# Output projection of the last but one attention unit: pairs of parts and seven products in place of plain matmuls

## The chip, the cores and the metric

The kernel runs on one core of a Trainium2 chip. The metric is the device time of one execution in microseconds; the median of several runs is given. The core has five engines with a queue each, worked in order: TensorE (PE; its weight loads are shown apart as PEld), VectorE (DVE), ScalarE (ACT), GpSimd (POOL) and SyncE (SP), which issues most DMAs. Everything is float32.

## The reference

One transformer layer with a norm after each half, on x of shape (2, 512, 512): grouped attention with 32 query heads, 8 key and value heads of width 128, rotary positions and a causal mask, then a feed-forward half that is a base matrix with a mixture of low-rank experts.

```python
q = hidden_states @ Wq + bq            # 32 heads of 128
k = hidden_states @ Wk + bk            # 8 heads
v = hidden_states @ Wv + bv
q, k = _rope(q, pos), _rope(k, pos)
scores = einsum('bgrsd,bgtd->bgrst', qg, k) / sqrt(128)
probs = softmax(where(causal, scores, min))
ctx = einsum('bgrst,bgtd->bgrsd', probs, v)
x = _layernorm(x + ctx @ Wo + bo)
y = x @ W_base.T + b_base
contribs = einsum('bter,eor->bteo', x @ A[active], Bm[active]) * 2
alpha = softmax(log(prior) + logits)   # router
x = _layernorm(x + y + sum_e contribs * alpha)
```

The change concerns `ctx @ Wo`, summed over the heads.

## The kernel before

**Units, parts, slots.** The attention is cut into 16 units, one for each pair of key head and batch element (4 query heads each), and each unit into 4 parts of 128 query rows: 64 parts, numbered p, four a unit. Parts 56 to 59 are unit 14, the last but one; parts 60 to 63 are unit 15, taken in the order of rows 2, 3, 0, 1. A part is worked in four slots, one score matmul each: slot T belongs to part T // 4, so there are 256 score slots. The function `slot(T)` writes out, by hand and in order, what every engine does in slot T. The schedule is manual: each engine takes its instructions in exactly that order, and semaphores order the engines among each other. Functions put in the table `extra` by `put(slot, f)` come at the end of their slot, in the order in which they were put there.

**What a part goes through.** Scores on TensorE (`score`, slot T); masked maximum on VectorE and exponentials on ScalarE one slot later; reciprocal, normalising and the transposes into `zt` up to slot T + 4; the transposed blocks are stored to DRAM (`blocks_out`, four DMAs on SP at slot 4p + 7) and read back as `pT` (`blocks_in`, one DMA on SP at slot 4p + 9, waiting for those four to land). The weighing with v (`weigh`) starts at slot 4p + 12 and takes as many slots as the part has key blocks, one matmul each; ScalarE then writes the context `ctxT` (`context_out`). There are two score banks: a score needs the bank of the score two slots earlier, which is free when its exponentials are done.

**Wo by pairs.** For units 0 to 13 the product of context and Wo is taken for two parts at once: the 2 x 2 blocks of the pair (two parts by two halves of the heads) times the 2 x 2 blocks of Wo (two halves of the heads by two halves of the columns), with seven block products in place of eight (`wo_products`, steps 0, 1, 2, 3, 4, 6, 7 in slots 21 + 8k + step for pair k). They need sums of weight blocks (`wo_sums`, four for each set of weights, on VectorE; the third overwrites a block of Wo in place), and sums of context blocks (`ctx_sums`, four for each pair, on POOL, one buffer). The products go into two PSUM banks, wx and wy. After a step, VectorE adds 256 columns from a bank to `x_sb` (`wo_adds`, seven adds a pair), one slot after the step. Most steps add into a bank that still holds the sum of earlier steps, so a step waits until the add that reads the earlier state is done.

**Wo plainly.** For units 14 and 15 each part has four matmuls over 512 columns (`wo_mm`), two in each of two slots listed in `plain_at`, and then one add of 512 columns (`wo_out`). Parts 56 to 59 take slots 246 to 251, 253 and 254; part 60 takes 256 and 257, part 61 takes 261 and 262; parts 62 and 63 come in the code after the loop.

**What else lies there.** At slot 237 the memory of the projections is closed and that of the FFN (`ffn_pool`) opened. Between slots 237 and 262 the base weights are loaded and transposed, and the FFN of the first batch element is woven in: `stats` at 238, 239 and 245, inverse roots by Newton steps at 240 and 245 (`newton`: four small VectorE operations, then twelve small POOL operations), `centre` at 246 and 247 on VectorE, transposes at 248 and 249, the base product at 250 and 251 for the first tile, `logits` and `alphas` (the router's softmax) at 252, `low_rank` at 253, `finish` and `add` at 254; the same for the next tiles from 256 and 258. The last Wo load (`load_wo`, 1 MB on SP) is put in slot 246.

Of the kernel before, what the change touches and what calls it, by code (L numbers as in the profile page):

```python
# [9 lines left out]
F32 = mybir.dt.float32  # L10
# [19 lines left out]
def postln_layer_kernel(  # L30
# [33 lines left out]
    nc = tc.nc  # L64
    B, S, HID = x.shape
    NT = B * S // P
    TPB = S // P
# [20 lines left out]
    NSETS = len(sets)  # L88
# [4 lines left out]
    def set_of(u):  # L93
        return u // B if u < MIXED else MIXED // B + u - MIXED
# [294 lines left out]
    def k_mm(u, c):  # L389
        g, b = unit(u)  # L390
        proj_mm(("k", u), ps_k, "k", wqk["k", g], slice(0, D), b, c)
# [43 lines left out]
    def strassen_sums(engine, a11, a12, a21, a22, s1, s2, s4):  # L435

        engine.tensor_tensor(s1, a21, a22, ALU.add)  # L437
        engine.tensor_tensor(s2, s1, a11, ALU.subtract)
        engine.tensor_tensor(s4, a12, s2, ALU.subtract)
        engine.tensor_tensor(a21, a11, a21, ALU.subtract)  # L440
# [6 lines left out]
    def product(ps, wt, xt, start):  # L447

        for c in range(CH):
            nc.tensor.matmul(  # L450
                ps, lhsT=wt[:, c, :], rhs=xt[:, c, :], start=start and c == 0, stop=c == CH - 1,
                skip_group_check=True)
# [177 lines left out]
    wt = {}  # L630
# [3 lines left out]
    def wo_block(n, c_half, n_half):  # L634
        return wos[n][:, CH * c_half : CH * (c_half + 1), ts(n_half, NHALF)]

    def wo_sums(n, step):

        if step == 0:
            shape = [P, 3, CH, NHALF]  # L640
            if n == NSETS - 4:
                wt[n] = late["pool"].tile(shape, F32, name="wt_late")
            else:
                wt[n] = wow.tile(shape, F32, tag="wt", name=f"wt_{n}", bufs=1)
        t1, t2, t4 = (wt[n][:, m] for m in range(3))
        b11, b12, b21, b22 = (wo_block(n, c_half, n_half) for c_half in range(2) for n_half in range(2))
        nc.vector.tensor_tensor(
            *((t1, b12, b11), (t2, b22, t1), (b12, b22, b12), (t4, b21, t2))[step], ALU.subtract)

    def ctx_block(k, head, c_half):  # L650
        return ctxT[2 * k + head][:, CH * c_half : CH * (c_half + 1), :]

    def ctx_sums(k):
        c = cs[k] = work.tile([P, 3, CH, P], F32, tag="cs", name=f"cs_{k}", bufs=1)
        strassen_sums(
            nc.gpsimd, *(ctx_block(k, h, c_half) for h in range(2) for c_half in range(2)), *(c[:, n] for n in range(3)))

    def wo_products(k, step):
        n = set_of(parts[2 * k][0])
        if step == 0:  # L660
            pw[k, "x"] = ps_wo.tile([P, NHALF], F32, tag="wx", name="wx")
            product(pw[k, "x"], ctx_block(k, 0, 0), wo_block(n, 0, 0), True)
        elif step == 1:
            pw[k, "y"] = ps_wo.tile([P, NHALF], F32, tag="wy", name="wy")
            product(pw[k, "y"], ctx_block(k, 0, 1), wo_block(n, 1, 0), True)
        elif step == 2:
            product(pw[k, "x"], cs[k][:, 1], wt[n][:, 1], False)
        elif step == 3:
            product(pw[k, "y"], cs[k][:, 0], wt[n][:, 0], True)
        elif step == 4:  # L670
            product(pw[k, "x"], ctx_block(k, 1, 0), wo_block(n, 0, 1), False)
        elif step == 6:
            product(pw[k, "x"], ctx_block(k, 1, 1), wt[n][:, 2], False)
        elif step == 7:
            product(pw[k, "y"], cs[k][:, 2], wo_block(n, 1, 1), False)

    def wo_add(k, bank, head, n_half):
        u, i = parts[2 * k + head]
        into = x_sb[:, unit(u)[1] * TPB + i, ts(n_half, NHALF)]
        nc.vector.tensor_tensor(into, pw[k, bank], into, ALU.add)  # L680

    def wo_adds(k, step):
        for bank, head, n_half in {
            1: (("x", 0, 0),), 2: (("y", 0, 0),), 3: (("x", 0, 1),), 4: (("y", 1, 1),),
            5: (("x", 1, 1),), 7: (("x", 1, 0),), 8: (("y", 0, 1),),
        }.get(step, ()):
            wo_add(k, bank, head, n_half)

    def wo_mm(p, r):

        u, i = parts[p]
        if r == 0:
            pwo[p] = ps_wo.tile([P, HID], F32, tag=("wx", "wy")[p % 2], name="po")
        nc.tensor.matmul(  # L694
            pwo[p], lhsT=ctxT[p][:, r, :], rhs=wos[set_of(u)][:, r, :], start=(r == 0), stop=(r == R - 1))
# [180 lines left out]
    NP = len(parts)  # L876
# [3 lines left out]
    LAG_WO = 21  # L880
    LAST = QB * TPB * (NU - 2)
# [3 lines left out]
    def put(slot, f):  # L885
        extra.setdefault(slot, []).append(f)
# [36 lines left out]
    late = {}  # L923
# [10 lines left out]
    def kv_at(T):  # L934

        frame, o = divmod(T - KV_FROM, UNIT)
        p, k = divmod(frame + B, VG * B)
        kind, b = "kv"[k // B], k % B
        if 0 < p < G // VG and (kind, p, b) != ("v", 1, 0):
            return (kind, p, b), o  # L940
        return None, None
# [16 lines left out]
            weigh_at.setdefault(QB * p + LAG_CTX + j + (p == NP - 2), []).append((p, j))  # L958


    plain_at = {}
    free = LAST + LAG_WO + 1
    for p in range(NP - 2 * TPB, NP):
        free = max(free, QB * p + LAG_CTX + parts[p][1] + 2)
        for step in range(2):
            plain_at[free + step] = p, step
        free += 2

    def slot(T):

        uq, step = divmod(T + 24, UNIT)
        kq, step = divmod(step, 8)
        now = 0 < uq < NU
        if now and step != 7 and step != 4:
            q_products(uq, kq, {0: 2, 1: 6, 2: 5, 3: 7, 5: 4, 6: 3}[step])
        un, kn = (uq, 1) if kq == 0 else (uq + 1, 0)
        if un < NU and step == 7:
            q_products(un, kn, 1)
        uk, l = divmod(T + UNIT, UNIT)
        if 0 < uk < PLAIN_K and l < KC:  # L980
            k_mm(uk, l)
        kv, o = kv_at(T)
        if kv and o in KV_STEPS:
            kv_products(*kv, KV_STEPS[o])
        kw, sw = divmod(T - LAG_WO, 8)
        products = 0 <= kw < LAST // 8
        if products:
            wo_products(kw, sw)
        plain = plain_at.get(T)
        if plain:  # L990
            p, step_o = plain
            wo_mm(p, 2 * step_o)
            wo_mm(p, 2 * step_o + 1)
        if 0 <= T < T_END:
            score(T)
        for part, j in weigh_at.get(T, ()):
            weigh(part, j)

        if now and step in (0, 2, 4, 6):
            q_copy(uq, kq, ("p1", "u2", "u3", "c21")[step // 2])  # L1000
        if kv and KV_OUT.get(o) in KV_ON_ACT:
            kv_out(*kv, KV_OUT[o])
        for part, j in weigh_at.get(T - 1, ()):
            if j == parts[part][1]:
                context_out(part)

        if 0 <= T - 3 < T_END:
            normalise(T - 3)
        if 0 <= T - 1 < T_END:
            masked_max(T - 1)  # L1010
            exponentials(T - 1)
        if products:
            wo_adds(kw, sw)
        if sw == 0 and 0 < kw <= LAST // 8:
            wo_adds(kw - 1, 8)
        if now and step in (1, 5, 7):
            q_sum(uq, kq, {1: "p1", 5: "u3", 7: "u2"}[step])
        if kv and o in KV_OUT and KV_OUT[o] not in KV_ON_ACT:
            kv_out(*kv, KV_OUT[o])
        if 0 <= T - 2 < T_END:  # L1020
            reciprocals(T - 2)
        if 0 <= T - 4 < T_END:
            blocks_transposed(T - 4)
            if (T - 4) % QB == QB - 1:
                blocks_out((T - 4) // QB)
        if T % QB == 1 and 0 <= T // QB - 2 < NP:
            blocks_in(T // QB - 2)
        if 0 <= (T - LAG_WO + 1) // 8 < LAST // 8 and (T - LAG_WO + 1) % 8 == 0:
            ctx_sums((T - LAG_WO + 1) // 8)

        ur, sr = divmod(T + 24 - 7, UNIT)
        kr, sr = divmod(sr, 8)
        if 0 < ur < NU and sr < 6:
            q_rope(ur, 2 * kr + (sr < 3), sr % 3)
        k_slots = (4, 5, 6) if uk < PLAIN_K else (11, 13, 14) if uk < NU - 1 else (3, 5, 6)
        if 0 < uk < NU and l in k_slots:
            k_rope(uk, k_slots.index(l))
        if plain and step_o:
            wo_out(p)
        for f in extra.pop(T, ()):  # L1040
            f()
# [88 lines left out]
        slot(T)  # L1130
    proj_stack.close()
    ffn_pool = ctx.enter_context(tc.tile_pool(name="ffn", bufs=1))
    wb_sb = ffn_pool.tile([P, OC, HID], F32, name="wb_sb")
    wbT = ffn_pool.tile([P, KC, 2, WX_COLS], F32, name="wbT")
    nc.gpsimd.tensor_copy(wbT[:, :, 0, OH : OH + ARH], arT[:, :, :ARH])
# [184 lines left out]
```

## Time and profile before

| | |
|---|---|
| median of 3 runs | 817.26 us (816.86 to 817.88) |
| the profiled execution's own time | 816.9 us |
| its span, first to last instruction | 815.1 us |
| granted TensorE clock | 0.998 |
| TensorE, VectorE, ScalarE, POOL busy | 99%, 75%, 47%, 42% of the span |
| plain Wo in the profile: matmul records, adds | 64 records, 8 adds of 692 ns |
| Wo by pairs: adds of 256 columns | 420 ns each |
| context sums on POOL, 128x256 | 740 to 837 ns mean |

A float32 matmul leaves two records in the profile. The records of TensorE overlap[...]; the chain of work that ended last shows by how much each moves the time on, as start, length, engine, tile and number of records. In lists of instructions a bracket gives the idle time ahead of an instruction and what ended it. Tiles: wx and wy are the banks of Wo by pairs, po those of plain Wo, sc scores, pc the weighing, tp transposes, py the FFN.

### The profile page before, as it was taken

How to read it: one execution, taken by the hardware profiler on the slowest of the kernel's cores; microseconds unless marked ns; L12 is line 12 of the kernel's file. 1: busy time of each engine (PE TensorE's matmuls, PEld its weight loads, DVE VectorE, ACT ScalarE, POOL GpSimd, SP SyncE). 2: the span in 40 equal slices, each digit the busy share in tenths (PEclk: the TensorE clock that was granted, in tenths of full speed). 3: DMA queues.
4: the chain of work that ended last, by engine and by line, in shares of the span. 5: the costliest groups of instructions: out<-in, count | busy, mean ns of one | idle time of the engine just before them, and what ended most of it. 6: DMA issues, size and time to landing. Idle time of an engine off the chain costs nothing.

```text
span 815.1 us, 11389 instructions
## 1 busy us (share of the span) xinstructions
PE 807.0 (99%) x3457; PEld 609.7 (75%) x3457; DVE 609.8 (75%) x1978; ACT 384.9 (47%) x1074; POOL 338.6 (42%) x392
## 2 busy tenths in 40 slices
PE   9999999999999999999999999999999999999996
PEld 7887777777777778777777778777777878656575
DVE  4778877687879886787867876787888689973455
ACT  2355454444545454545435454544545454663244
POOL 8666645421444345322443245343464333420033
PEclk9999999999999999999999999999999999999999
DMA  9025736355455637264544637365453726674211
GB/s 298 26 72 143 219 83 202 91 130 156 134 169 136 182 93 219 77 181 129 147 147 121 178 82 219 91 160 179 137 146 91 232 66 181 189 263 143 77 39 65
DMA packets 84415, 116.00 MB, mean 142 GB/s; under 512 B 6525, under 2 KB 64237, under 8 KB 82306
## 3 DMA queue, kind: packets, MB, share of 16 engines
q1 hardware_dynamic: 83154, 114.71, 49.0%
q8 instruction: 27, 0.44, 0.2%
q10 hardware_dynamic: 752, 0.42, 0.2%
q14 instruction: 34, 0.28, 0.1%
q0 software_dynamic: 448, 0.14, 0.1%
HBM read 71.21 MB, written 44.04 MB: 141 GB/s over the span
## 4 chain that ended last, share of the span: by engine, by line
PE 96%; POOL 1%; DVE 1%; ACT 1%; issue 0%; POOLq 0%
PE pc L618 17%; PE sc L562 15%; PE qx L450 14%; PE wx L450 12%; PE qy L450 10%; PE wy L450 9%; PE kx L450 4%; PE vx L528 4%; PE po L694 3%; PE py L788 3%; PE pv L348 3%; PE pp L365 1%; PE tp L285 1%; PE py L829 1%; POOL zt L191 0%; POOL act_er L220 0%
## 5 line engine op out<-in xcount | busy, mean ns | idle before, releaser
L577 ACT ACTIVATE p<-sc,nmax 128x288 f32<-128x288 f32 (+15 forms) x256 | 124.2, 485 | 197.7 <-DVE nmax L570 175.2
L570 DVE CUSTOM_DVE_ANT_0 sc<-sc,maskw 128x288 f32<-128x288 f32 (+15 forms) x256 | 114.2, 446 | 136.3 <-PE sc L562 134.7
L618 PE MATMUL pc<-pT,v 128*128 128x512 f32 x320 | 165.3, 599 | 0.0
L562 PE MATMUL sc<-kT,qT 128*128 128x160 f32 (+15 forms) x512 | 161.7, 398 | 0.3 <-ACT p L577 0.3
L386 POOL TENSOR_TENSOR qT<-q,t 128x512 f32<-128x512 f32 x64 | 88.0, 1376 | 176.1 <-DVE q L385 165.0
L585 ACT ACTIVATE p<-p,den 128x288 f32<-128x288 f32 (+15 forms) x256 | 133.2, 521 | 0.0
L562 PEld LDWEIGHTS sc<-kT,qT 128*128 128x128 f32 x512 | 96.1, 190 | 21.9 <-issue 8.1
L625 ACT ACTIVATE ctxT<-pc,bqkT 128x512 f32<-128x512 f32 x64 | 44.0, 688 | 114.8 <-PE pc L618 114.7
L437 POOL TENSOR_TENSOR cs<-ctxT 128x256 f32<-128x256 f32 x28 | 22.4, 801 | 158.5 <-PE wy L450 95.4
L593 DVE STREAM_TRANSPOSE zt<-p 128x128 f32<-128x128 f32 (+2 forms) x192 | 81.7, 426 | 0.0
L486 ACT COPY q<-qx 128x256 f32<-128x256 f32 x128 | 47.4, 370 | 51.4 <-PE qx L450 49.8
L618 PEld LDWEIGHTS pc<-pT,v 128*128 128x128 f32 x320 | 57.1, 190 | 18.7 <-issue 5.7
L450 PE MATMUL qx<-xs,wq 128*128 128x256 f32 x256 | 66.3, 381 | 0.0
L450 PEld LDWEIGHTS qx<-xs,wq 128*128 128x128 f32 x256 | 47.3, 190 | 23.2 <-issue 18.4
L595 DVE STREAM_TRANSPOSE zt<-p 128x32 f32<-128x32 f32 (+3 forms) x256 | 57.6, 225 | 0.0
L450 PE MATMUL wx<-wo,ctxT 128*128 128x256 f32 x224 | 57.5, 379 | 0.0
L378 DVE SCALAR_TENSOR_TENSOR t<-q,bqkT,rope_sb 64x512 f32<-64x512 f32 x64 | 52.3, 818 | 3.5 <-ACT q L486 1.7
L381 DVE SCALAR_TENSOR_TENSOR t<-q,bqkT,rope_sb 64x512 f32<-64x512 f32 x64 | 50.3, 786 | 1.5
L577 ACT ACTIVATION_READ_ACCUMULATOR p<-sc,nmax 128x1 f32 x256 | 49.8, 194 | 0.0
L385 DVE SCALAR_TENSOR_TENSOR q<-q,bqkT,rope_sb 128x512 f32<-128x512 f32 x64 | 48.1, 751 | 0.1
L450 PEld LDWEIGHTS wx<-wo,ctxT 128*128 128x128 f32 x224 | 42.5, 190 | 7.0 <-issue 1.4
L680 DVE TENSOR_TENSOR x_sb<-wx,x_sb 128x256 f32<-128x256 f32 x112 | 47.0, 420 | 0.0
(234 smaller groups left out, 1468.3 us busy)
## 6 DMA issues: line engine op xcount, KB each, us to landing
db<-zt SPq DMA_DIRECT2D x64, 256.0 KB, 4.3
pT<-db SPq DMA_DIRECT2D x16, 1024.0 KB, 4.8
db<-zt SPq DMA_DIRECT2D x64, 192.0 KB, 3.3
pT<-db SPq DMA_DIRECT2D x16, 768.0 KB, 4.4
wq<-in_L_attn_Wq_dram SPq DMA_DIRECT2D x20, 512.0 KB, 5.1
wo<-in_L_attn_Wo_dram SPq DMA_DIRECT2D x10, 1024.0 KB, 9.0
db<-zt SPq DMA_DIRECT2D x64, 128.0 KB, 2.4
pT<-db SPq DMA_DIRECT2D x16, 512.0 KB, 4.2
```

What stands on the lines that cost most here:

```text
L378: nc.vector.scalar_tensor_tensor(t2[lo, :], q[hi, :], b_ap[hi, :], rope_sb[hi, 1, :], ALU.add, ALU.mult)
L381: nc.vector.scalar_tensor_tensor(t2[hi, :], q[lo, :], b_ap[lo, :], rope_sb[lo, 1, :], ALU.add, ALU.mult)
L385: nc.vector.scalar_tensor_tensor(t1, q, b_ap, rope_sb[:, 0, :], ALU.add, ALU.mult)
L386: nc.gpsimd.tensor_tensor(dst, t1[:, :].rearrange("p (n s) -> p n s", s=BLK), t2[:, :].rearrange("p (n s) -> p n s", s=BLK), ALU.add)
L450: nc.tensor.matmul(ps, lhsT=wt[:, c, :], rhs=xt[:, c, :], start=start and c == 0, stop=c == CH - 1, skip_group_check=True)
L562: nc.tensor.matmul(sc[s][:, :w], lhsT=qT[u][:, i * QB + n].rearrange("p r s -> p (r s)"), rhs=kT[u][:].rearrange("p n s -> p (n s)")[:, :w ...
L570: nc.vector.tensor_tensor_reduce(sc[s][:, :w], sc[s][:, :w], maskw[:, S - w :], -SCALE, -MASKED, ALU.add, ALU.min, nmax[s])
L577: nc.scalar.activation(ptile[s][:, :w], sc[s][:, :w], AF.Exp, bias=nmax[s], scale=-1.0, accum_out=rden[s])
L585: nc.scalar.activation(ptile[s][:, :w], ptile[s][:, :w], AF.Copy, scale=rden[s])
L593: nc.vector.transpose(z[:, :, last - i : last, n, :].rearrange("p q j s -> p j q s"), ptile[s][:, : i * P])
L595: nc.vector.transpose(z[:, : n + 1, last, n, :], ptile[s][:, i * P : w])
L618: nc.tensor.matmul(psc[p], lhsT=v_sb[g // VG, b][:, j, ts(g % VG, D)], rhs=pT[p][:, :, ts(j, P)], start=(j == 0), stop=(j == i))
```

## The change

Unit 14 (parts 56 to 59, two pairs, numbers 28 and 29) takes Wo by pairs too.

- The plain products and adds of parts 56 to 59 go away; `plain_at` keeps parts 60 to 63. Part 60 moves from slots 256 and 257 to 257 and 258; part 61 stays.
- Pair 28 takes slots 247 to 251 with one step each (0 to 4) and slot 252 with steps 6 and 7. Pair 29 takes slot 253 with steps 0 and 1, 254 with 2 and 3, 255 with 4, 256 with 6 and 7.
- For these two pairs, `wo_adds` come in the same slot as their step; for the earlier pairs they come one slot after it, as before.
- `ctx_sums` of the two pairs, four POOL operations each, are put at slots 246 and 252.
- `wo_sums` of unit 14's weights, four operations, are put on POOL at slots 242, 243, 245 and 246, into a tile `wt_last` of the FFN's memory. As they are put earlier in the code, they stand ahead of what other functions put in the same slot; in slot 245 that is the second `newton`, and in slot 246 the context sums come ahead of the fourth weight sum.
- The steps of the earlier pairs are now read from a table (`wo_at`, `adds_at`) and keep their slots.

```diff
-    def wo_sums(n, step):
+    def wo_sums(n, step, engine=nc.vector):
...
+            elif n == NSETS - 2:
+                wt[n] = late["ffn"].tile(shape, F32, name="wt_last")
...
-        nc.vector.tensor_tensor(
+        engine.tensor_tensor(
             *((t1, b12, b11), (t2, b22, t1), (b12, b22, b12), (t4, b21, t2))[step], ALU.subtract)
...
+    WO_PAIRS = (NP - TPB) // 2
+    wo_at = {}
+    for k in range(WO_PAIRS - 2):
+        for step in (0, 1, 2, 3, 4, 6, 7):
+            wo_at[8 * k + LAG_WO + step] = (k, (step,))
+    LAST_PAIRS = LAST + LAG_WO + 2
+    for n, steps in enumerate(((0,), (1,), (2,), (3,), (4,), (6, 7))):
+        wo_at[LAST_PAIRS + n] = (WO_PAIRS - 2, steps)
+    for n, steps in enumerate(((0, 1), (2, 3), (4,), (6, 7))):
+        wo_at[LAST_PAIRS + 6 + n] = (WO_PAIRS - 1, steps)
+
+    adds_at = {}
+    for T, (k, steps) in wo_at.items():
+        for step in steps:
+            adds_at.setdefault(T + (k < WO_PAIRS - 2), []).append((k, step + 1))
+    for n in range(2):
+        put(LAST_PAIRS + 6 * n - 1, lambda n=n: ctx_sums(WO_PAIRS - 2 + n))
+    for step in range(4):
+        put(LAST_PAIRS + (-5, -4, -2, -1)[step], lambda step=step: wo_sums(NSETS - 2, step, nc.gpsimd))
+
     plain_at = {}
-    free = LAST + LAG_WO + 1
-    for p in range(NP - 2 * TPB, NP):
+    free = LAST_PAIRS + 10
+    for p in range(NP - TPB, NP):
         free = max(free, QB * p + LAG_CTX + parts[p][1] + 2)
...
-        kw, sw = divmod(T - LAG_WO, 8)
-        products = 0 <= kw < LAST // 8
-        if products:
-            wo_products(kw, sw)
+        kw, steps_w = wo_at.get(T, (0, ()))
+        for step_w in steps_w:
+            wo_products(kw, step_w)
...
-        if products:
-            wo_adds(kw, sw)
-        if sw == 0 and 0 < kw <= LAST // 8:
-            wo_adds(kw - 1, 8)
+        for k, read in adds_at.get(T, ()):
+            wo_adds(k, read)
...
     ffn_pool = ctx.enter_context(tc.tile_pool(name="ffn", bufs=1))
+    late["ffn"] = ffn_pool
```

## The prediction

> **What bounds the kernel now.** I read the page first, for each engine's busy time, then the chain of work that ended last around the changed slots, then the timelines of SP, VectorE and POOL there. Page:
>
> ```profile
> PE 807.0 (99%) x3457; PEld 609.7 (75%) x3457; DVE 609.8 (75%) x1978; ACT 384.9 (47%) x1074; POOL 338.6 (42%) x392
> ```
>
> TensorE is never free, so its work and its waits make the time. The chain shows what a piece of work costs there (start, length, what); the slots that change begin at 721.71:
>
> ```profile
> 711.73 0.86 PE wx L450 x4
> ...
> 721.71 1.72 PE po L694 x4
> 723.42 0.81 PE sc L562 x2
> 724.23 0.86 PE pc L618 x2
> 725.09 0.44 PE tp L285 x4
> 725.53 1.72 PE po L694 x4
> 727.24 0.86 PE sc L562 x2
> 728.10 1.72 PE po L694 x4
> 729.82 0.14 PE sc L562 x2
> 729.96 0.94 PE pc L618 x2
> ```
>
> One product of a pair is 0.86 us (four records); half a plain part is 1.72, so a part is 3.44. In this stretch every piece begins where the one before ended: here TensorE alone set the pace. The slots can be read off: 246 starts at 721.71, 247 at 725.53, 248 at 728.10; further down the same view, 249 at 731.77, 252 at 744.74, 255 at 752.70, 256 at 753.13.
>
> **The change, part by part.**
>
> *TensorE's work.* Removed: 4 plain parts x 3.44 = 13.76 us. Added: 2 pairs x 7 products x 0.86 = 12.04. Balance -1.72 us, which is -0.21% of 815.1. That is the whole prize; whatever wait appears comes off it.
>
> *Where the work lies.* Before, slots 246 to 251, 253 and 254 each held 1.72 of plain product, and 256 and 257 held part 60. After: 246 nothing; 247 to 251 one product (0.86); 252, 253, 254 two (1.72); 255 one; 256 two; part 60 in 257 and 258. So TensorE first runs ahead of the old schedule by 1.72 + 0.86 + 0.86 = 3.44 us at the end of slot 248's products, by more until 251, and pays it back from 252 on. Running ahead is where it can meet data that is not there. I walked each slot with the old durations and asked which partner is late.
>
> *First wait: slot 248, the load of pT for part 59.* Without waits: slot 246 is 0.81 + 0.86 + 0.44, to 723.82; slot 247 is 0.86 + 0.86, to 725.54; slot 248's product ends at 726.40, its score at 726.54. Then the weighing of part 59 needs its pT. SP issues that load here:
>
> ```profile
> 723.24 0.34 SPq L611 DMA_DIRECT2D pT<-db  x1
> 723.67 0.40 SPq L162 DMA_DIRECT2D wo<-in_L_attn_Wo_dram  x1
> ```
>
> ```profile
> pT<-db SPq DMA_DIRECT2D x16, 1024.0 KB, 4.8
> ```
>
> The load is issued once part 59's block stores (issued at 716.73, slot 243, before anything changed) have landed; nothing in the change moves it forward. It lands at 723.24 + 4.8 = 728.04. Before, the weighing began at 729.96 and never saw it; now TensorE waits 728.04 - 726.54 = 1.5 us. [...] I take the row, a load of the same size on the same queue[...]. ScalarE's exponentials of slot 246, which free the score bank of 248, end near 726.5 by their old lengths (wb copy, context, normalising, exponentials), 0 to 0.3 us late, inside this wait.
>
> *The middle, 249 to 254.* Weighing 59 now starts 729.96 - 728.04 = 1.92 us ahead of the old time. Slots 249 to 251 save 0.86 each (4.50 ahead at 252), 252 gives back 1.72 (2.78 ahead at 253 and 254). Part 60's load was issued at 734.65, lands in 4.3, so by 739.0, or 0.6 later because one extra add precedes its stores on VectorE; needed at 742.2. Part 61's stores follow an add at 737.8 and go out at about 738.8 against 738.44 before, its load lands near 750, needed near 754. Both hidden, by 2.6 and 4 us.
>
> *POOL.* Added: 4 weight sums on 128x512 and 8 context sums on 128x256. The rows nearest to the first have the same shape and engine:
>
> ```profile
> L429 POOL TENSOR_TENSOR xs<-xT x2: 1275/1494/1712, 29.3 to 32.2; 128x512 f32<-128x512 f32 x2
> L429 POOL TENSOR_TENSOR xs<-xT,xs x2: 1598/1688/1779, 30.7 to 36.4; 128x512 f32<-128x512 f32 x2
> ```
>
> So 1.3 to 1.8 each; the context sums are 0.73 to 0.93 (3.2 a pair in the timeline, gaps included). The first three weight sums stand ahead of the second Newton root of the norms:
>
> ```profile
> 722.66 0.20 POOL L737 TENSOR_TENSOR t<-rstd_a 128x2 f32<-128x2 f32 x1 [6.91 <-DVE rstd_a L735]
> ```
>
> POOL was idle for 6.91 us there; 3 x 1.8 = 5.4 fit, so Newton still starts at 722.66 and ends at 726.35. Pair 28's context sums follow to 729.6, the fourth weight sum to 731.4. Step 2 (slot 249, at 729.85) needs the second context sum, done near 728.1; step 6 (slot 252, about 740) needs the fourth weight sum. [...] Newton's steps beside the two centrings at 723.62 took 0.38 instead of 0.20. The other two centrings (0.99 us) will meet the context sums[...]. Uncovered, each us is a us. Pair 29's context sums start after step 7 of pair 28 (ends near 741.9), second done by 743.7, needed at 746.1. The new tile lies in memory whose last projection user on POOL ended at 706.9, so I cost it nothing; if it had to wait, the bound is POOL's same 1.5 us of spare before Newton slips.
>
> *VectorE's adds.* 14 x 0.42 = 5.9 us for 4 x 0.69 = 2.8: +3.1 us on an engine that idled up to 3.44 us at a time before these plain adds. Hidden as work, +3.1 if not. Their place matters more: from pair 28 on, a slot's adds come in the same slot, and the next product into that bank waits for them. Pair 29 packs two steps a slot, so one add stands between slots with the FFN's work ahead of it in VectorE's order.
>
> *Second wait: slot 256.* Step 6 of pair 29 adds into the bank that step 4 (slot 255) filled, so it waits for that bank's add, and ahead of it on VectorE are the finish of the first FFN tile (slot 254) and slot 254's masked maximum:
>
> ```profile
> 752.30 0.86 DVE L839 TENSOR_TENSOR y<-py,x_sb 128x256 f32<-128x256 f32 x2 [0.98 <-PE py L829]
> 753.20 0.69 DVE L713 BATCH_NORM_STATS2 st<-y 128x6 f32<-128x512 f32 x1
> ...
> 754.02 0.37 DVE L570 CUSTOM_DVE_ANT_0 sc<-sc,maskw 128x224 f32<-128x224 f32 x1
> ```
>
> The finish's matmuls start at 751.84 in the chain; VectorE has done the maximum at 754.31, 2.47 later, and the add would end 0.42 later, 2.89 after. Now the finish starts 2.78 earlier, at 749.06; the add ends at 751.95. TensorE is through the finish (0.86), step 4 (0.86) and the score (0.43) at 751.21, so it waits 0.74, plus 0.05 for the signal and 0.2 of restart (a product that had waited for such an add took 1.07 instead of 0.86, at 708.87): 1.0 us. Queued behind it on TensorE: step 7, the weighing and the FFN base, so all later work.
>
> *Sum.* -1.72 + 1.5 + 1.0 = **+0.8 us**. After 258 the old order returns and TensorE stays full to 801, so no later gap absorbs it. Profiled execution: span 815.1, to 815.9. Its own time was 816.9, 1.8 above its span; the median 817.26 is 2.16 above. The prediction moves the median: 817.26 + 0.8 = **818.1**.
>
> **Rivals.**
> *All of the gain:* pT lands early and the add is in time. For it: TensorE was the only limit before. Against: the load's issue and the add's place above. 817.26 - 1.7 = 815.5.
> *One wait only:* the load's, 817.1, or the add's, 816.5. For it: both margins, 1.5 and 0.7 us, are sums of many short pieces.
> *A third wait, slower than before:* slot 254, step 2 of pair 29 needs the add of step 0, which stands behind the router's softmax of the first tile (1.45 us from 744.78 to 746.23 in the old timeline, with a ScalarE step in it) and behind the last add of pair 28. I get that add done near 744.9 and TensorE there at 746.1: 1.2 us to spare. From 1.2 late on it decides; an equal slip again costs 1.2, 819.3.
> *It changes nothing because other work hides TensorE:* excluded by the 99%.
>
> **How the numbers follow.** 0.2% is 1.63 us, about what a measurement of this kernel can tell from no change: the bounds are 815.63 and 818.89. Chances: two waits 0.52 (own range 817.4 to 819.0), one wait 0.20, all gained 0.05, a third wait or longer ones 0.23. Faster: the 0.05. Slower: the 0.23 and 0.04 from the upper end of the two-wait case. Same: the rest, 0.68. The range leaves out the full gain and the far end of the third wait: 816.2 to 820.0.
>
> **What would show it.** Right: fourteen 0.86 products and no plain product before part 60; a TensorE wait on the pT load near 726.5 of about 1.5 us, one on the x_sb add near 751 of about 1 us; Newton still starting near 722.7. Wrong: no wait at either place, weight sums over 2.3 us each that push Newton back, or a wait on POOL's sums at steps 2 or 6.

## The result, and the profile after

| | before | after |
|---|---|---|
| median | 817.25 us (816.83 to 817.94, 15 runs) | 819.31 us (817.74 to 824.38, 15 runs) |
| ratio of the medians, 95% interval | | 1.003 (1.0017 to 1.0044) |
| profiled execution, span | 815.1 us | 822.6 us |
| granted TensorE clock there | 0.998 | 0.994 |

The change costs 2.1 us. The forecast was 818.1, the range 816.2 to 820.0. The shortest execution of after, 817.74, is 0.9 above the shortest of before, close to the forecast step of 0.8; the median is 1.2 above the forecast value. The spread belongs to the result: before, 15 executions lay within 1.1 us, after they lie within 6.6. The clock sorts them without exception: the eight executions with a mean granted clock of 0.998 or more took 817.74 to 819.31, the seven with 0.997 or less took 820.25 to 824.38. So the median is the longest execution of the first group. The profiled one is the longest of all, so the lines below show the costs at their largest.

Busy times, on the page:

```profile
PE 809.7 (98%) x3481; PEld 617.2 (75%) x3481; DVE 612.6 (74%) x1988; ACT 384.9 (47%) x1074; POOL 349.0 (42%) x404
```

TensorE's busy time is up by 2.7 us, although 1.72 us of work were taken away: part of its work ran longer. The chain of work that ended last shows where (start, length, what):

```profile
723.66 0.77 PE pc L618 x2
724.43 6.89 DMA pT<-db
...
731.37 2.07 PE pc L618 x2
733.44 1.71 PE tp L285 x8
735.15 1.71 PE wx L450 x4
...
755.64 0.45 PE py L831 x2
...
758.26 0.29 DVE x_sb L682
758.59 1.13 PE wx L450 x4
```

Before, the chain ran through this stretch on TensorE alone. Now it leaves TensorE twice. First it passes through the load of pT for part 59, which takes 6.89 us from issue to landing; the weighing behind it, the transposes and the product of slot 249 take 2.07, 1.71 and 1.71 us. Then it passes through VectorE, from the finish of the first FFN tile to the add of 256 columns that step 6 of pair 29 needs. TensorE's timeline, with the idle time and its releaser in the bracket, gives both waits their sizes:

```profile
731.37 2.07 PE L618 MATMUL pc<-pT,v 128*128 128x512 f32 x2 [3.57 <-DMA pT<-db]
...
758.59 1.13 PE L450 MATMUL wx<-wt_last,ctxT 128*128 128x256 f32 x4 [0.80 <-DVE x_sb L682]
```

Why the pieces behind the first wait run long is in the table by stretches of 1 us (window, length, busy share and instructions of PE, PEld, DVE, ACT, POOL, then the granted clock, DMA share, GB/s):

```profile
729.00:730.00 1.00, 0.00 (x0) 0.00 (x0) 1.00 (x5) 0.21 (x1) 1.00 (x2) 1.00 0.85 193
730.00:731.00 1.00, 0.00 (x0) 0.00 (x0) 0.81 (x6) 0.56 (x2) 1.00 (x2) 0.86 0.75 205
731.00:732.00 1.00, 0.63 (x1) 0.50 (x2) 0.00 (x0) 0.00 (x0) 0.57 (x1) 0.50 1.04 393
...
736.00:737.00 1.00, 1.00 (x6) 0.82 (x4) 0.11 (x1) 0.63 (x3) 0.00 (x0) 0.50 0.02 8
737.00:738.00 1.00, 1.00 (x3) 0.56 (x3) 1.00 (x5) 0.00 (x0) 0.00 (x0) 0.72 0.35 49
```

TensorE has been idle since 727.8. In the window from 730 the granted clock begins to drop to one half, and in the one from 737 it comes back. Read in stretches of 0.1 us, the clock is 1.00 up to 730.7, 0.50 from 730.8 to 737.5 and 1.00 again from 737.6; taken as either whole or half, 0.86 means half for 0.28 us and 0.72 for 0.56 us; with the six windows at 0.50 between them that is 6.84 us at half clock. A row of the whole execution fits: 3.4 us lost in 822.6 is 0.004, and the mean clock is 0.994 where it was 0.998. TensorE had been idle for 2.92 us, from 727.80 to 730.72, when the clock fell. Whether the length of a wait decides that is weighed below, with more waits.

The span grew by 7.5 us. Its parts, from the two traces: 0.93 of a later start that lies ahead of every changed slot (in the traces of other edits of the changed kernel it is 0.1 to 1.0, so it differs between executions); 0.22 in slot 244, where the weighing of part 58 found its pT late by a little; -1.72 of products; 3.57 of the first wait and 0.27 of restart behind it (a weighing of 1.13 instead of 0.86); 3.0 of the half clock (five pieces took 2.07, 1.71, 1.71, 0.32 and 1.16 us, and 1.13, 0.87, 0.86, 0.17 and 0.91 in a trace with a wait and no fall); 1.07 of the second wait with its restart. That is 7.3.

POOL's timeline, and after it VectorE's two centrings of slot 247, the line from before first:

```profile
723.59 0.19 POOL L739 TENSOR_TENSOR t<-rstd_a 128x2 f32<-128x2 f32 x1 [3.07 <-DVE rstd_a L737]
...
727.22 0.72 POOL L437 TENSOR_TENSOR cs<-ctxT 128x256 f32<-128x256 f32 x1
728.02 0.79 POOL L438 TENSOR_TENSOR cs<-cs,ctxT 128x256 f32<-128x256 f32 x1
```

```profile
727.89 0.99 DVE L743 TENSOR_SCALAR x_sb<-x_sb,mv_a,rstd_a 128x512 f32<-128x512 f32 x2
...
727.30 1.79 DVE L745 TENSOR_SCALAR x_sb<-x_sb,mv_a,rstd_a 128x512 f32<-128x512 f32 x2 [0.28 <-POOL rstd_a L742]
```

The weight sums cost POOL 1.3 us each (the first ran from 716.62 to 717.92) and it still idled 3.07 us ahead of Newton. But the two centrings, 0.99 us before, now take 1.79 beside the context sums. In this trace TensorE waits for the load then, and the delay costs nothing; it comes back below.

### The profile page after: what moved, and what is told of

Read it like the earlier page. It is cut to its first block, busy times and chain, and to the rows that moved or that the text cites. A ratio compares the mean times of both kernels' runs of the same rounds, so it can differ in the third digit from the quotient of the medians.

```text
span 822.6 us, 11464 instructions
## 1 busy us (share of the span) xinstructions
PE 809.7 (98%) x3481; PEld 617.2 (75%) x3481; DVE 612.6 (74%) x1988; ACT 384.9 (47%) x1074; POOL 349.0 (42%) x404
## 4 chain that ended last, share of the span: by engine, by line
PE 96%; DVE 2%; DMA 1%; ACT 1%; issue 0%; SPq 0%; DVEq 0%
PE pc L618 17%; PE sc L562 14%; PE qx L450 13%; PE wx L450 12%; PE qy L450 10%; PE wy L450 9%; PE kx L450 4%; PE vx L528 4%; PE py L790 3%; PE pv L348 3%; PE po L696 2%; PE pp L365 1%; PE tp L285 1%; DMA pT<-db 1%; DMA x_sb<-_attn_hidden_states_dram 0%; PE py L831 0%
## 5 line engine op out<-in xcount | busy, mean ns | idle before, releaser
L450 PE MATMUL wx<-wo,ctxT 128*128 128x256 f32 x240 | 61.6, 379 | 0.0
L682 DVE TENSOR_TENSOR x_sb<-wx,x_sb 128x256 f32<-128x256 f32 x120 | 50.4, 420 | 11.8 <-PE wx L450 11.8
L450 PEld LDWEIGHTS wx<-wo,ctxT 128*128 128x128 f32 x240 | 45.4, 190 | 7.8 <-issue 1.7
```

The lines of the kernel that those rows point to most:

```text
L450: nc.tensor.matmul(ps, lhsT=wt[:, c, :], rhs=xt[:, c, :], start=start and c == 0, stop=c == CH - 1, skip_group_check=True)
```

## The experiments

The texts on record name theories by letters. **D**: the pT load of part 59 is late because it shares the DMA engines with the Wo load issued right behind it. **P**: POOL's sums disturb another engine, and that makes the spread. **C**: the clock falls by itself. **W**: TensorE, ahead of its old schedule, meets a load that it never saw before; the idle time, and the fall of the clock in some executions, are the whole spread. **S** (from the ninth run on): with the load's wait gone, the score of slot 249 waits for the slowed centrings. Each set of runs has the kernel before beside it, and its median is given too; the two are compared within a set, since medians of one kernel differ between sets.

### The changed kernel again

No edit.

> The changed kernel as it is, for a second trace beside the edits. Theory D (the load of pT for part 59 lands late because it shares the DMA engines with the Wo load issued right behind it, and TensorE, idle for some 3 us, then runs at half clock for some 6 us): times spread as before from 817.7 to over 820, and in each trace the end of the wait at slot 248 is the landing of that load; a trace with a landing about 4.8 us after the issue has a span near 816 and no fall of the clock there, one with 6 to 7 us has the fall. Theory P (POOL's sums disturb VectorE or the stores, and these the load): the same spread, but with VectorE's operations or the stores ahead of the load longer in the slow traces. Theory C (the clock falls by itself): a fall also in traces with an early landing.

Measured: 821.69 us (820.24 to 822.48, 5 runs) against 817.58; ratio 1.0053 (1.004 to 1.0066). In this set the change costs 4.1 us and the median lies outside the forecast range. The five clocks are 0.994 to 0.997. The chain of its trace, with the weighing's line from TensorE's timeline in its place:

```profile
719.28 5.66 DMA db<-zt
...
725.01 4.83 DMA pT<-db
...
729.89 1.30 PE L618 MATMUL pc<-pT,v 128*128 128x512 f32 x2 [2.31 <-DMA pT<-db]
...
731.19 1.71 PE tp L285 x8
732.89 1.54 PE wx L450 x4
```

This load took 4.83 us, what the prediction used, but it was issued late, because the stores ahead of it landed 5.66 us after their issue. The wait was 2.31 us. The stretches, in the columns of the table of the result; the three between them, from 731 to 734, have 0.50:

```profile
730.00:731.00 1.00, 1.00 (x3) 0.34 (x4) 0.71 (x4) 0.47 (x2) 1.00 (x2) 0.86 0.90 322
...
734.00:735.00 1.00, 1.00 (x6) 0.73 (x5) 0.53 (x3) 0.38 (x3) 0.00 (x0) 0.94 1.05 390
```

By the same reckoning 0.28 + 3 + 0.12 = 3.40 us at half clock. TensorE was idle for 2.31 us at most before it, and had been at work again for 0.8 us when the clock fell at 730.72. The three pieces cost 4.55 us instead of 2.86: 1.7 us for the fall.

### The Wo load moved away from the pT load

```diff
-        put(wo_from(set_units(n - 2)[-1] + 1) + 1, lambda n=n: load_wo(n))
+        put(249 if n == NSETS - 1 else wo_from(set_units(n - 2)[-1] + 1) + 1, lambda n=n: load_wo(n))
```

> Only the last Wo load is moved, from slot 246 (right behind the pT load of part 59 on SP) to slot 249 (behind the pT load of part 60). Theory D: the pT load lands 4.2 to 4.8 us after its issue in every execution, the spread goes, the wait at slot 248 is 1.0 to 1.6 us, no fall of the clock: median 817.8 to 818.2, that is +0.6 to +0.9 against before. Theory P or C: the spread from 818 to 824 stays, median near 819.3.

Measured: 821.34 us (818.05 to 823.5, 6 runs) against 817.58; ratio 1.0047 (1.0029 to 1.0065). The chain, again with the weighing's line from the timeline:

```profile
724.37 4.76 DMA pT<-db
...
729.18 1.13 PE L618 MATMUL pc<-pT,v 128*128 128x512 f32 x2 [1.60 <-DMA pT<-db]
...
730.30 0.87 PE tp L285 x8
731.18 0.86 PE wx L450 x4
```

In the profiled execution the load took 4.76 us, the wait was 1.60 and the clock didn't fall: the forecast first wait, nearly to the tenth. But the six executions spread nearly as widely as the fifteen of the changed kernel, with clocks from 0.994 to 0.999, where D had forecast 817.8 to 818.2 and no spread. The Wo load behind the pT load isn't what makes the spread.

### The Wo load ahead of the pT load

The same line with slot 244 in place of 249.

> The last Wo load is moved the other way, to slot 244, ahead of the pT load of part 59 on SP. Theory D: 1 MB more stands ahead of it, so the stores of part 59 or the load land some 2 to 5 us later, the wait at slot 248 grows to 4 to 8 us, the clock falls in every execution: 822 to 828. Theory P or C: the load's place doesn't matter, 819.3 as it was.

Measured: 823.56 us (823.28 to 824.37, 4 runs) against 817.58; ratio 1.0074 (1.006 to 1.0089). The chain and the timeline have

```profile
724.91 7.25 DMA pT<-db
...
732.21 2.07 PE L618 MATMUL pc<-pT,v 128*128 128x512 f32 x2 [4.80 <-DMA pT<-db]
```

With the Wo load in front of it, the pT load takes 7.25 us, the wait is 4.80, and every execution shows a clock of 0.993 or 0.994. So a load ahead can delay this one: 7.25 us against 4.76 with the Wo load out of the way, one trace each (6.89 came with none ahead), and all four executions are long. As the cause of the spread, D is wrong. And with the long wait in every execution the spread is down to 1.1 us.

### The finish of the first FFN tile one slot later

```diff
-            put(at + 4, lambda f=f: (f.finish(), f.add()))
+            put(at + 4 + (f is f0[0]), lambda f=f: (f.finish(), f.add()))
```

> Only the finish and add of the first FFN tile are moved, from slot 254 to slot 255, behind the add that step 6 of pair 29 waits for. My account of the second wait (step 6 waits for the x_sb add, which stands behind that finish on VectorE): the wait of about 1 us at slot 256 is gone, so 1.0 us off the median of the changed kernel, the spread stays: 818.3 or so, fast ones near 817.0. Rival (VectorE is full there, the wait only moves to another product): no gain, 819.3.

Measured: 818.39 us (816.89 to 823.26, 22 runs) against 817.58; ratio 1.0016 (1.0007 to 1.0026). The chain, where the finish (py) now comes behind step 4 (wx) and a score:

```profile
751.25 0.86 PE wx L450 x4
752.12 0.43 PE sc L562 x2
752.55 0.86 PE py L831 x4
753.41 0.86 PE wx L450 x4
```

Every piece begins where the one before ends: the second wait is gone. The shortest execution falls from the first set's 817.74 to 816.89, by 0.85 us; 0.80 of wait and 0.27 of restart stood there. The medians within this set, 821.69 and 818.39, can't price it: five of five executions of the changed kernel have a clock of 0.997 or less, nine of 22 here. The long executions stay, which is as it should be: the first wait was not touched. In the profiled one it is longer than the 2.31 us of the second trace, yet the clock stayed whole:

```profile
730.01 1.12 PE L618 MATMUL pc<-pT,v 128*128 128x512 f32 x2 [2.52 <-DMA pT<-db]
```

**The clock fell with a wait of 2.31 us and not with one of 2.52.** In the columns of the table of the result, first four windows of this section's trace, then two of the trace with the Wo load ahead; the six between those two, from 730 to 736, have 0.50:

```profile
728.00:729.00 1.00, 0.00 (x0) 0.00 (x0) 1.00 (x3) 0.00 (x0) 0.92 (x2) 1.00 0.94 389
729.00:730.00 1.00, 0.00 (x0) 0.00 (x0) 1.00 (x5) 0.41 (x1) 1.00 (x2) 1.00 0.80 152
730.00:731.00 1.00, 0.99 (x3) 0.47 (x4) 0.62 (x4) 0.37 (x2) 1.00 (x2) 1.00 0.74 240
731.00:732.00 1.00, 1.00 (x10) 1.00 (x9) 0.00 (x0) 0.40 (x1) 0.39 (x1) 1.00 1.08 287
...
729.00:730.00 1.00, 0.00 (x0) 0.00 (x0) 1.00 (x5) 0.46 (x1) 1.00 (x2) 0.90 0.90 364
...
736.00:737.00 1.00, 1.00 (x4) 0.79 (x4) 0.00 (x0) 0.98 (x2) 0.00 (x0) 0.69 0.87 350
```

In this section's trace every window from 727 to 738 has 1.00. With the Wo load ahead the reckoning gives 0.20 + 6 + 0.62 = 6.82 us at half clock, beside 6.84 and 3.40 in the two traces of the changed kernel. The falls lie differently to the waits: 2.92 us into the wait in the first trace of the changed kernel, 2.39 us into it with the Wo load ahead (from 727.41 to 729.80), 0.83 us behind its end in the second. From 727 to 730 TensorE was busy for 0.80, 0.41 and 0.69 us in these three, and for 0.48 us in the trace without a fall. So neither the length of the wait nor TensorE's work in these three microseconds decides alone; what else does, these traces don't show.

### The weighing of part 59 one slot later

```diff
-            weigh_at.setdefault(QB * p + LAG_CTX + j + (p == NP - 2), []).append((p, j))
+            weigh_at.setdefault(QB * p + LAG_CTX + j + (p == NP - 2) + (p == NP - 5 and j == 0), []).append((p, j))
```

> The changed kernel, with the first weighing of part 59 moved from slot 248 to slot 249, so that TensorE comes to it 1.9 us later (two transposes of a tile, one product, one score come first); nothing is added or left out. Theory W (TensorE is ahead of the pT load, and its idle time there, with the clock that falls in some executions when it is idle, is the whole of the spread): the wait of 1.5 to 3.6 us falls to 0 to 1 us, hardly any fall of the clock, so 1.5 us or more off the fast executions and no slow ones: median 816.6 (817.26 - 1.72 + 1.0), spread under 1.5 us. Theory P (POOL's sums or the added VectorE work make the spread): the spread from 818 to 823 stays.

Measured: 818.55 us (817.65 to 818.96, 21 runs) against 817.49; ratio 1.0011 (1.0005 to 1.0018). This takes the wait for the load away and leaves all else in place, POOL's sums included, and the spread is gone: 21 executions within 1.3 us, all clocks but one 0.998 or 0.999. That decides between W and P. But the median missed W's 816.6: the shortest execution gained only 0.09 us, where 1.5 to 2 were to be had. The timeline, VectorE's line first, then TensorE's:

```profile
727.41 1.79 DVE L745 TENSOR_SCALAR x_sb<-x_sb,mv_a,rstd_a 128x512 f32<-128x512 f32 x2 [0.29 <-POOL rstd_a L742]
...
728.98 1.13 PE L450 MATMUL wx<-wt_last,cs 128*128 128x256 f32 x4 [0.27 <-POOL cs L438]
...
730.74 0.43 PE L562 MATMUL sc<-kT,qT 128*128 128x64 f32 x2 [0.63 <-ACT p L577]
```

Two waits stand where the load's was. Step 2 waits for its context sum, and the score of slot 249 waits for the exponentials that free its bank. They wait for the masked maximum on VectorE, and that stands behind the two slowed centrings. The load's wait had covered both.

### Both of these edits

> As e5_weigh_later, and the finish of the first FFN tile one slot later as in e2_finish_later: both waits gone. Theory W and my account of the second wait: nothing is left but the work saved, 817.26 - 1.72 = 815.5 to 815.9, faster than before by 0.16 to 0.2%. If the waits are turned into new ones elsewhere: 816.5 to 817.5.

Measured: 817.13 us (816.51 to 817.72, 13 runs) against 817.49; ratio 0.9998 (0.999 to 1.0006). The edit of the finish is worth 1.42 us of median here: the second wait with its restart, 1.07, and 0.35 that I can't place. The kernel is level with the one before, not at the 815.5 to 815.9 that W gave without new waits; its trace has the two waits of the last fence again, 0.31 and 0.63 us.

### The kernel before without the product of part 56

```diff
-            wo_mm(p, 2 * step_o)
-            wo_mm(p, 2 * step_o + 1)
+            if p != NP - 2 * TPB:
+                wo_mm(p, 2 * step_o)
+                wo_mm(p, 2 * step_o + 1)
```

The add of the part is left out too.

> The kernel before, with the plain product and add of part 56 left out (four matmuls, 3.44 us, in slots 246 and 247), so the output lacks that part. No pairs, no POOL sums, no added VectorE work; but TensorE is ahead of the pT load of part 59 by as much as in the changed kernel. Theory W: of the 3.44 us only some 1.9 are gained in the fast executions (1.5 go into the wait), 815.3, and the spread of the changed kernel appears, to 819 or more; the trace shows the wait at slot 248 and in slow executions the clock at half. Theory P: 813.8, no spread.

Measured: 816.06 us (814.98 to 819.09, 22 runs) against 817.49; ratio 0.9989 (0.9982 to 0.9995). This is the old kernel with TensorE set ahead by 3.44 us and none of the new products and sums on POOL. TensorE's timeline:

```profile
727.97 1.12 PE L618 MATMUL pc<-pT,v 128*128 128x512 f32 x2 [1.06 <-DMA pT<-db]
```

The same wait, at the same instruction. Of 3.44 us of work taken away, 1.43 reach the median; 1.06 and 0.27 go into the wait and its restart in the profiled execution. Five of 22 executions have a clock of 0.997 and take 817.94 to 819.09, the tail of the changed kernel in small. Neither POOL nor the seven products are needed for the spread: being early at this load is enough. P falls, and C too: the kernel before has no clock below 0.997 in any execution beside these runs, and its three of 0.997 took 817.55 to 817.8, no longer than the others. Four other executions of it took 819.5 to 820.6 with a clock of 0.998 or 0.999; that rare lengthening has another cause, which no trace here shows.

### Four unread matmuls ahead of the weighing of part 59

```diff
+        if T == LAST + LAG_WO + 3:
+            fill = ps_q.tile([P, TH], F32, tag="qx", name="fill")
+            for _ in range(4):
+                nc.tensor.matmul(fill, lhsT=ident, rhs=bmT[:, :TH], start=True, stop=True)
```

> The changed kernel with four matmuls of 256 columns (1.72 us of work that nobody reads) ahead of the score of... that is, ahead of the weighing of part 59 in slot 248. Theory W with the clock: TensorE is busy while the load comes in, so the wait shrinks from 1.5-3.6 us to 0-1.8 and the clock falls seldom: fast executions about 818.2 as before, the slow ones over 820 gone, median 818.0 to 818.6. If the clock has no part in it and only the landing counts: the slow executions stay wherever the landing is late, median 819 and up. Theory P: 1.72 us more than the changed kernel, 821.

Measured: 820.25 us (818.63 to 822.6, 5 runs) against 817.49; ratio 1.0041 (1.0028 to 1.0053). The forecast of W, 818.0 to 818.6, missed, and the run is inconclusive. In the profiled execution the load landed at 728.62; the filler's matmuls ran from 726.61 to 728.58, so they filled the wait almost to the end. Four clocks are 0.998 or 0.999, the fifth has 0.996 and took 822.6. But five executions can't separate this from the changed kernel's eight in fifteen, and two of the four took 820.25 and 820.44, longer than any execution of the changed kernel's first set with such a clock (819.31 at most); what held them up no trace shows.

### POOL's work in another order

On top of both edits: the context sums of pair 28 two slots earlier, ahead of the third weight sum and Newton, and the fourth weight sum put two slots later.

```diff
-        put(LAST_PAIRS + 6 * n - 1, lambda n=n: ctx_sums(WO_PAIRS - 2 + n))
+        put(LAST_PAIRS + (-3, 5)[n], lambda n=n: ctx_sums(WO_PAIRS - 2 + n))
...
-        put(LAST_PAIRS + (-5, -4, -2, -1)[step], lambda step=step: wo_sums(NSETS - 2, step, nc.gpsimd))
+        put(LAST_PAIRS + (-5, -4, -2, 1)[step], lambda step=step: wo_sums(NSETS - 2, step, nc.gpsimd))
```

> As e6_weigh_finish_later, and on POOL the context sums of pair 28 go ahead of the second Newton root (slot 244, into the 3 us that POOL is idle) and the fourth weight sum goes to slot 248, so that no POOL sum but that one can meet the two centrings of VectorE. Theory S (with the load's wait gone, the score of slot 249 waits some 1.3 us for a chain of centring, masked maximum and exponentials, of which 0.8 us is the centring slowed by POOL's context sums beside it): the two centrings take 1.0 us instead of 1.8, the product that waited 0.8 us for POOL's second sum waits no more, the score of slot 249 waits 0.5 us or less: 0.8 to 1.3 us off, median 815.9 to 816.4. Rival (VectorE's load itself sets the chain, POOL has no part): 817.1 as without it.

Measured: 817.97 us (817.32 to 818.57, 14 runs) against 817.63; ratio 1.0005 (0.9997 to 1.0013). A miss: not faster than without the new order; by the medians it is 0.84 us slower, or 0.70 with each taken against the kernel before beside it, and the intervals overlap. The timeline, POOL and VectorE:

```profile
722.33 1.28 POOL L649 TENSOR_TENSOR wo<-wo 128x512 f32<-128x512 f32 x1
722.97 0.67 DVE L733 TENSOR_SCALAR v<-mv_a 128x2 f32<-128x2 f32 x1
...
727.91 1.95 DVE L745 TENSOR_SCALAR x_sb<-x_sb,mv_a,rstd_a 128x512 f32<-128x512 f32 x2 [0.29 <-POOL rstd_a L742]
```

The collision had moved, not gone. The third weight sum now ran beside the first small operation of Newton on VectorE, 0.67 us instead of 0.17, so POOL's part of Newton began at 724.19 instead of 723.51. The fourth weight sum came at 727.83 all the same: POOL waited for nothing and ran ahead of the slot in which I had put it. Beside its 1.29 us the centrings took 1.95. The score of slot 249 waited 1.46.

### The late centrings out of the chain

On top of that: the third and fourth centring in slot 248 instead of 247, behind the masked maximum that the score of 249 needs, and all three matmuls of the weighing of part 59 in slot 250.

```diff
-        put(A + 1 + k // 2, f.centre)
+        put(A + 1 + k // 2 * 2, f.centre)
...
-            weigh_at.setdefault(QB * p + LAG_CTX + j + (p == NP - 2) + (p == NP - 5 and j == 0), []).append((p, j))
+            weigh_at.setdefault(QB * p + LAG_CTX + j + (p == NP - 2) + (p == NP - 5) * max(0, 2 - j), []).append((p, j))
```

> As e9_pool_order, and the other two centrings one slot later (248), so that the masked maximum of slot 247 is not behind Newton's last step, and the first three weighings of part 59 all in slot 250. Theory S and W: no wait is left at slots 248 to 250 and none at 256, TensorE saves its 1.72 us: median 815.5 to 815.9, spread as before's. If the moved centrings make the transposes of slot 249 wait: 816.3 to 817.

Measured: 816.38 us (815.5 to 816.9, 22 runs) against 817.63; ratio 0.9981 (0.9974 to 0.9987). The chain:

```profile
728.87 0.87 PE wx L450 x4
729.74 0.17 PE sc L562 x2
...
731.85 2.60 PE pc L618 x6
```

The score of slot 249 begins when TensorE is through with the product ahead of it. S holds in this: with the centrings out of the way in VectorE's order the wait is gone. How much of it was their place and how much their slowness no run separates; the 0.80 us of slowing is more than the wait of 0.63. This kernel is 1.25 us faster than the one before, and the first whole kernel whose interval lies below it; some 0.5 of the 1.72 is still missing, and the forecast of 815.5 to 815.9 with it. One short wait is left in the trace: the score of slot 248 waits 0.24 us for its exponentials.

### The late centrings with POOL's first order

The kernel of the last experiment with both lines of POOL's order put back.

> The kernel of e10 with POOL's order put back to that of the changed kernel: context sums of pair 28 in slot 246 behind Newton, fourth weight sum in slot 246 behind them. Kept from e10: the late weighing of part 59, the late finish of the first FFN tile, and the third and fourth centring in slot 248. If the moved POOL order itself harms (first Newton operation on VectorE 0.64 instead of 0.17 beside the third weight sum, so that Newton starts some 0.5 late and the score of slot 248 waits), this kernel is faster than e10 by 0.2 to 0.5: 815.9 to 816.2, with product step 2 waiting at most 0.3 for its context sum. If the gain of e10 came from both moves together, the centrings still meet POOL's sums in slot 247 or 248 and the score of slot 249 waits again: 816.8 to 817.2, as without the moved centrings.

Measured: 816.47 us (815.56 to 817.03, 21 runs) against 817.32; ratio 0.9987 (0.998 to 0.9994). That is neither of the two forecasts, but the same time as with POOL's new order: with the centrings out of the chain, the order on POOL makes no difference that these runs can tell. Two lines of the timeline show what is left:

```profile
728.20 1.40 DVE L745 TENSOR_SCALAR x_sb<-x_sb,mv_a,rstd_a 128x512 f32<-128x512 f32 x2
...
728.49 1.13 PE L450 MATMUL wx<-wt_last,cs 128*128 128x256 f32 x4 [0.31 <-POOL cs L438]
```

The centrings still meet POOL, 1.40 us, now without cost. Step 2 waits 0.31 for its context sum and loses 0.27 in the restart, two thirds of the 0.87 us that this kernel is short of the full gain.

### The weight sums behind Newton

From the kernel of the last but one experiment: the third and fourth weight sum both behind Newton, the context sums ahead of it.

```diff
-        put(LAST_PAIRS + (-5, -4, -2, 1)[step], lambda step=step: wo_sums(NSETS - 2, step, nc.gpsimd))
+        put(LAST_PAIRS + (-5, -4, -1, -1)[step], lambda step=step: wo_sums(NSETS - 2, step, nc.gpsimd))
```

> The kernel of e10 with the third weight sum moved behind Newton (slot 246) and the fourth after it in the same slot; the context sums of pair 28 stay in slot 244, ahead of Newton. That leaves two short waits of the earlier runs without their cause: the one of product step 2 for its context sum (0.31 and a restart of 0.27, in the kernel with POOL's old order) and the late start of Newton (first operation 0.64 instead of 0.17) that holds the score of slot 248 for 0.24. If those are what is left of the gain, 815.7 to 816.1 and no wait of TensorE for POOL in slots 247 to 250. If the third and fourth weight sum, now beside the centrings of slot 248, hold VectorE so long that the masked maximum behind them delays the score of slot 250, 816.4 or more.

Measured: 816.22 us (815.82 to 817.02, 17 runs) against 817.6; ratio 0.9985 (0.9978 to 0.9992). Not to be told from the last two, and just above the forecast 815.7 to 816.1. TensorE's waits for POOL are gone, as meant, and one of 0.63 has come in their place:

```profile
728.47 1.95 DVE L745 TENSOR_SCALAR x_sb<-x_sb,mv_a,rstd_a 128x512 f32<-128x512 f32 x2
...
730.11 1.08 PE L285 MATMUL tp<-ident,x_sb 128*128 128x128 f32 x8 [0.63 <-ACT p L585]
```

The first of these centrings took 1.49 us beside the weight sums and ended at 729.96; the transposes of that tile begin 0.15 later. The trace names ScalarE's normalising as the releaser, which the transposes have no use for; that it was the centring is read from the order and the times, not shown. The three arrangements are 0.3 to 0.9 us short of the full gain; in each trace a wait of 0.24 to 0.63 us stands where POOL's sums met VectorE or came late.

## Why the prediction was right, and where it was not

- **TensorE's work, -1.72 us.** Right. The products took 0.86 us each, and the kernels whose waits were taken away came to 0.9 to 1.4 below the one before, with short waits of 0.24 to 0.63 us left in their traces.
- **The first wait.** Right in its place, instruction and cause, and in the profiled execution with the Wo load moved also in its size (1.60 for 1.5). The term was mis-sized: I took one landing time, 4.8 us from one row, for an event that varies. In six traces the stores ahead took 4.3 to 6.2 us to land, the load took 4.63 to 7.25, and before the change 1.9 us of cover stood in front of that. The waits measured are 1.06 to 4.80. The restart behind the wait, 0.27, was left out, though the sum has one behind the second wait.
- **What the step left out: the clock.** A wait was priced at its own length. Where TensorE idled at this load, the granted clock fell to 0.50 in three traces, and the three pieces behind it cost 1.7 to 2.6 us more, in one of them 3.0 with the next two. The prediction gives the clock nothing, without a reason. The runs show that the length alone does not decide it: waits of 1.06, 1.60 and 2.52 left the clock whole, 2.31, 3.57 and 4.80 did not. What else decides was not shown.
- **The second wait, 1.0 us.** Right in its place, its chain through VectorE and its size: 0.80 and 0.27, and 0.85 to 1.42 when it was taken away.
- **POOL, counted as no wait.** The first half held: Newton began no later than the whole stretch (723.59, with the 0.93 us of the later start), with 3.07 us of POOL idle ahead of it. The second half, that no sum comes late, held only under cover of the load's wait. I let the centrings meet the context sums and looked for the cost on POOL. The trace shows the other engine paying: the sums stay at 0.72 to 0.79, while VectorE's two centrings go from 0.99 to 1.79. And I had asked what POOL's sums would hold up, but not what stands behind the centrings on VectorE: the masked maximum, the exponentials and the score of slot 249.
- **The middle slots and the loads of parts 60 and 61.** Right: no wait on them.
- **The rivals.** The time is what the third one gave, 819.3, and outside the two-wait case's own 817.4 to 819.0, though not by the third one's mechanism: slot 254 had no wait. It was the "longer ones" that this case named in its chance. The whole gain (815.5) was not reached; with other work moved as well, the medians came to 816.2 to 816.5.
- **Luck.** That the median lies in the range is in part luck. It is the longest of the eight executions with a clock of 0.998 or more; with one more among the slower ones it would have been 820.25, above the range, and in the second set of the same kernel it was 821.69.

Open: why the block stores and the load land late in some executions and not in others. The load landed latest with the Wo load ahead of it; with that moved away the spread remained.

## What to carry to other kernels

Taking work from the engine that sets the time moves it ahead of everything timed against it; list each transfer and partner that it now meets early, with its margin, and take the margin against the slowest landing that the traces show, not the middle one. Price a wait on TensorE as idle time plus a possible half clock behind it: here 1.7 us where it lasted 3.40 us and 3.0 where it lasted 6.84, in a stretch where TensorE set the pace. The mean clock changed from execution to execution, 0.994 to 0.999 in fifteen of one kernel, so look at the spread and not only at one trace. And when a wait is removed, look for what it had covered: here a second engine's slowdown, worth nearly as much, lay under it.

## What the runs showed of the hardware that I had not expected

- A granted TensorE clock of 0.50 after a wait of 2.31 us in one execution, and of 1.00 after 2.52 us in another. In the three traces with a fall at this load the half clock lasted 3.40, 6.82 and 6.84 us.
- Where VectorE met POOL's sums, VectorE lost most: two centrings of 128x512 took 0.99 us alone, 1.40 to 1.95 beside them; an operation on 128x2 took 0.67 instead of 0.17; a context sum took 0.73 alone and 0.79 beside (once 0.92). It is not always VectorE: POOL's small Newton steps took 0.38 instead of 0.20 beside two centrings of 0.96. In two cases the one that began later took longer: the operation on 128x2 began at 722.97 behind a sum of 722.33 to 723.61 and ended at 723.64; before, the Newton step of 0.38 began at 723.79 behind a centring of 723.62.
- The same 1 MB load on the same queue took 4.63 to 7.25 us from issue to landing; in the changed kernel alone, two executions gave 4.83 and 6.89, both with the Wo load right behind it.
